# The routing's chain laid out in one piece, and long VectorE work of the attentions ordered behind its end

## The chip, the core and the metric

The kernel runs on one core of a Trainium2 chip. The metric is the device time of one execution in microseconds. A core has five engines that concern us: TensorE (PE in the profile, with its weight loads as PEld), VectorE (DVE), ScalarE (ACT), GpSimd (POOL) and SyncE (SP), which here only issues transfers. Each engine works through a queue of its own, fixed when the program is built.

## What is computed

Four macaron layers run over a residual stream of 4 batches of 1024 tokens with 128 channels, all in float32: half a feed-forward, an attention, the other half of the feed-forward. Layers 0 and 2 have a mixture of experts as their feed-forward, and these are where the change works. Cut to what matters:

```python
# layer 0; layer 2 is alike with relu and a router bias
logits = einsum('td,ed->te', layernorm(x), router_w)
top_vals, top_idx = top_k(logits, 2)                # 8 experts, two for each token
probs = softmax(top_vals)
out += probs[e] * (gelu(x @ w1[e].T + b1[e]) @ w2[e].T + b2[e])   # for the two chosen
x = x + 0.5 * out
# layer 0's attention: for each token, 16 heads of 8 channels attend to each other
scores = einsum('bshd,bstd->bsht', Q, K) / sqrt(8)
x = x + (softmax(scores) @ V) @ Wfc.T
# layer 2's attention: a linear recurrence over time with decay gamma
s = gamma * s + k_t v_t^T ; z = gamma * z + k_t ; y_t = q_t s / (q_t z + eps)
```

So a token's second routing (after the attention) can't be computed before its attention is done, and its attention not before its first experts are done.

## The kernel before

**Experts.** Only the chosen experts are computed. The tokens of a group of batches are sorted by expert into blocks of 128 slots: 23 blocks for a group of one batch, 39 for a group of two. For each block, `experts` (line 424) has SP load the expert's weights (0.58 MB, tile e_w, 4 buffers), has POOL gather the 128 tokens (L457, tile e_xg, 6 buffers), turns them on PE (L461), copies them on VectorE (L463, e_x), multiplies up, applies the activation on ScalarE (L468, e_h), multiplies down, adds the bias on VectorE (L441, e_y) and has POOL scatter the rows to DRAM (L442, res). `combine` (L476) loads the two rows of each token back (c_y), weighs them and adds them to the residual.

**Routing.** `route` (L276) says which token goes to which slot. It has a part for each batch (centring, squares, logits: L287 to L312), then a chain of small VectorE operations, each of which needs the one before: the two greatest logits (`top`, L321, tiles g_m to g_pick), counts per expert (L339 to L373), then, for 8 tokens of 128 at a time (g_lanes, L399), a comparison on VectorE and matmuls on PE that sum up which token stands in which slot (g_cols, held), and last g_source (L409), which the gathers read, and g_target (L412), which the scatters read. For two batches this chain is 50 VectorE instructions.

**Groups.** Layer 0 has six routings: batches (0), (1), (2,3) before the attention, (0,1), (2), (3) after it, with 23, 23, 39, 39, 23 and 23 blocks. Layer 2 has four of two batches each. I number the 326 blocks through: layer 0's second round begins with block 86, after (0), (1) and (2,3); its later groups begin with 125 and 148; layer 2's groups begin with 171, 210, 249 and 288. The routing of a group has to be done before its first block.

**Layout.** The functions are Python generators. `lanes` runs one lane of tasks for the experts, one for the combines, one or two for the rest, and always continues the lane whose clock is lowest; each `yield n` moves that lane's clock on by n. What stands in one stretch between two yields is laid out together. The order of layout is not yet the order on the engines: the framework's scheduler, which runs when the program is built, puts each engine's instructions in order by its own estimate of when each is ready, and prefers what was laid out earlier. After that the order on each engine is fixed, and semaphores wait where data come from another engine. A manual dependency marked NoSync adds only an order for the scheduler, no wait in the program.

In `route`, the first part yields 8 after each batch, and the chain yields 3, 5, 3, then 1 for each group of lanes, and 2 at the end, so that it can be interleaved with the other lanes' tasks.

**The attentions.** `l0_attn` (L501) works through 8 steps of 128 tokens per batch. A step has four long VectorE operations over 2048 elements per partition: q times k (L528, prod), the sum over channels (L530, sc), weights times values (L545, prod) and the sum over the attended heads (L547, o), and some six short ones. I call these four the long operations; layer 0 has 4 x 8 x 4 = 128 of them. `l2_attn` (L878) has shorter ones (kv L894, at L901, den L917).

## Time and profile before

| | |
|---|---|
| median of 3 runs | 3209.11 us (3207.99 to 3214.21) |
| the profiled execution | 3296.3 us, span of its instructions 3294.4 us |
| mean granted TensorE clock in it | 0.905 of full speed |
| busy: PE, VectorE, ScalarE, POOL | 2875.3, 1826.5, 1649.2, 807.0 us |
| layer 0 with its experts | about 0 to 940 us of the span |
| layer 1's attention | about 940 to 2040 us |
| layer 2 with its experts | about 2100 to 2790 us |
| layer 3 | from about 2790 us |

The profiled execution is 2.7% longer than the median run, so times read in it are compared with each other and with its own span. Percentages of busy time are averages over stages that have different limits; a stretch of the span is judged by what its engines do in it.

Where each group of blocks stands in the profiled execution (the end of g_target L412, the start of the first e_x L463, the end of the last e_y L441):

| group | blocks | g_target ends | first e_x | last e_y |
|---|---|---|---|---|
| layer 0, (0) | 1 to 23 | 46.8 | 50.0 | 144.7 |
| (1) | 24 to 46 | 79.0 | 142.8 | 235.4 |
| (2,3) | 47 to 85 | 177.7 | 232.6 | 386.7 |
| second round, (0,1) | 86 to 124 | 514.6 | 516.9 | 670.1 |
| (2) | 125 to 147 | 643.8 | 667.4 | 783.2 |
| (3) | 148 to 170 | 791.4 | 797.3 | 897.5 |
| layer 2, (0,1) | 171 to 209 | 2153.9 | 2159.3 | 2291.4 |
| (2,3) | 210 to 248 | 2215.3 | 2289.6 | 2450.9 |
| second round, (0,1) | 249 to 287 | 2476.2 | 2479.6 | 2646.8 |
| (2,3) | 288 to 326 | 2649.7 | 2653.9 | 2780.8 |

### The profile page before, as it was taken

The page shows a single profiled execution, that of the slowest core. Times are in us where ns is not written, and L with a number is a line of the kernel's source. Part 1 is how long each engine was busy: PE and PEld are TensorE (multiplying, and loading weights), DVE is VectorE, ACT ScalarE, POOL GpSimd, SP SyncE. Part 2 cuts the span into 40 slices and gives each one's busy share as a digit, 9 for nine tenths or more (in the row PEclk, how much of TensorE's full clock was granted, in tenths as well). Part 3 has the DMA queues.
Part 4 walks back from the last instruction along what each step waited for, and adds up shares of the span by engine and source line. Part 5 has one row for each costly group of instructions (what it writes and reads, how often), then busy time and mean ns, then how long its engine had stood idle before and what let it go on. Part 6 is the DMA issues. An engine that isn't in the chain of part 4 may idle for free.

```text
span 3294.4 us, 48535 instructions
## 1 busy us (share of the span) xinstructions
PE 2875.3 (87%) x18206; PEld 1685.8 (51%) x18206; DVE 1826.5 (55%) x3160; ACT 1649.2 (50%) x3640; POOL 807.0 (24%) x748
## 2 busy tenths in 40 slices
PE   6888637878879999999999999988988977899997
PEld 6766426766643333333333333586777865344333
DVE  3376877774226676676776772431555521355664
ACT  3565524658613565566566565444444534444442
POOL 2565405552340000000000000046434454011110
PEclk7989858889977999999999999979989988788997
DMA  4766414663500000000000000157565666000000
GB/s 151 227 186 188 140 42 130 185 188 115 168 9 7 4 6 4 6 6 4 21 5 6 1 1 9 42 152 245 171 185 147 199 197 194 0 0 0 7 7 13
DMA packets 122890, 277.64 MB, mean 84 GB/s; under 512 B 18016, under 2 KB 67296, under 8 KB 122528
## 3 DMA queue, kind: packets, MB, share of 16 engines
q1 hardware_dynamic: 101792, 231.77, 23.8%
q0 software_dynamic: 20864, 42.77, 4.3%
q8 instruction: 144, 2.36, 0.3%
q14 instruction: 90, 0.74, 0.1%
HBM read 238.43 MB, written 31.85 MB: 82 GB/s over the span
## 4 chain that ended last, share of the span: by engine, by line
PE 74%; DVE 12%; ACT 5%; issue 4%; DMA 3%; POOL 1%; another core or an unknown queue 0%; SPq 0%; ACTq 0%; DVEq 0%; POOLq 0%
PE bank L227 40%; PE two L227 17%; PE o L227 8%; PE s L227 4%; DVE nm L720 2%; ACT e_h L468 2%; PE wave L1010 1%; DVE prod L545 1%; PE bank L461 1%; DMA c_y<-res 1%; DVE sc L530 1%; ACT L468 1%; DMA e_w<-in_l0m_dram 1%; DVE prod L528 1%; DVE e_x L463 1%
## 5 line engine op out<-in xcount | busy, mean ns | idle before, releaser
L720 DVE TENSOR_REDUCE nm<-two 128x2 f32<-128x1024 f32 x512 | 626.9, 1225 | 288.3 <-PE s L227 268.9
L743 ACT ACTIVATE e<-s 128x512 f32<-128x512 f32 x1024 | 556.4, 595 | 405.6 <-PE s L227 402.6
L468 ACT ACTIVATE e_h<-bank,e_w 128x128 f32<-128x128 f32 x1304 | 454.8, 368 | 511.6 <-PE bank L227 388.4
L227 PE MATMUL bank<-e_x,e_w 128*128 128x128 f32 x2608 | 569.3, 318 | 154.5 <-ACT e_h L468 79.9
L227 PE MATMUL s<-qm,kz 32*128 32x512 f32 x2048 | 634.1, 643 | 0.8 <-ACT e L743 0.8
L227 PE MATMUL two<-kz,qz 32*128 32x512 f32 x2048 | 593.2, 664 | 21.3 <-DVE nm L720 2.5
L227 PEld LDWEIGHTS bank<-e_x,e_w 128*128 128x128 f32 x2608 | 413.9, 204 | 291.3 <-ACT e_h L468 144.4
L457 POOL DMA_INDIRECT e_xg<-rows,g_source x326 | 334.4, 1026 | 835.1 <-DVE g_target L412 354.2
L227 PE MATMUL bank<-e_w,e_h 128*128 128x128 f32 x2608 | 445.7, 291 | 12.3 <-ACT e_h L468 6.9
L442 POOL DMA_INDIRECT res<-e_y,g_target x326 | 373.5, 1146 | 337.0 <-DVE e_y L441 152.7
L227 PEld LDWEIGHTS bank<-e_w,e_h 128*128 128x128 f32 x2608 | 378.8, 205 | 23.0 <-ACT e_h L468 13.3
L227 PE MATMUL o<-e,va 128*32 128x256 f32 x4096 | 328.8, 392 | 0.1
L441 DVE TENSOR_TENSOR e_y<-bank,e_w 128x128 f32<-128x128 f32 x326 | 94.3, 290 | 403.7 <-PE bank L227 317.0
L227 PEld LDWEIGHTS two<-kz,qz 32*128 32x128 f32 x2048 | 159.7, 189 | 239.9 <-issue 164.0
L227 PEld LDWEIGHTS o<-e,va 128*32 128x32 f32 x4096 | 81.0, 108 | 390.3 <-issue 370.3
L227 PEld LDWEIGHTS s<-qm,kz 32*128 32x128 f32 x2048 | 206.9, 183 | 10.9 <-issue 7.7
L708 POOL COPY va<-vd 128x256 f32<-128x256 f32 x16 | 6.7, 433 | 626.3 <-PE o L227 538.0
L1115 POOL TENSOR_TENSOR z<-st,r 128x512 f32<-128x512 f32 x32 | 46.2, 1445 | 417.1 <-DVE st L1108 333.7
L463 DVE COPY e_x<-bank 128x128 f32<-128x128 f32 x326 | 93.0, 285 | 92.2 <-PE bank L461 67.6
L227 PE MATMUL bank<-g_cols,g_lanes 128*128 128x39 f32 (+1 forms) x512 | 90.5, 341 | 28.9 <-DVE g_cols L392 28.8
L461 PE MATMUL bank<-c,e_xg 128*128 128x128 f32 x326 | 95.0, 291 | 21.7 <-DMA e_xg<-rows,g_source 21.6
L227 PEld LDWEIGHTS bank<-g_cols,g_lanes 128*128 128x128 f32 x512 | 91.2, 270 | 32.5 <-issue 31.4
(300 smaller groups left out, 3694.0 us busy)
## 6 DMA issues: line engine op xcount, KB each, us to landing
e_w<-in_l0m_dram SPq DMA_DIRECT2D x170, 578.0 KB
e_w<-in_l2m_dram SPq DMA_DIRECT2D x156, 578.0 KB
c_y<-res SPq DMA_DIRECT2D x32, 512.0 KB
rows<-g_xt SPq DMA_DIRECT2D x16, 512.0 KB
e_xg<-rows,g_source POOLq DMA_INDIRECT x326
res<-e_y,g_target POOLq DMA_INDIRECT x326
x<-in_x_dram SPq DMA_DIRECT2D x4, 512.0 KB
qz<-qd SPq DMA_DIRECT2D x64, 32.0 KB
```

The costliest lines, as they stand in the source:

```text
L227: self.nc.tensor.matmul(out, lhsT, rhs, start=start, stop=stop)
L441: nc.vector.tensor_tensor(y, o, w[:, MOE_W - D :], ALU.add)
L442: ins = nc.gpsimd.indirect_dma_start(out=res[:, :], out_offset=at(target[:, k : k + 1]), in_=y, in_offset=None)
L457: nc.gpsimd.indirect_dma_start(out=xg, out_offset=None, in_=rows[:, :], in_offset=at(source[:, k : k + 1]))
L461: nc.tensor.transpose(tp, xg, self.c0["ident"])
L463: nc.vector.tensor_copy(x, tp)
L468: nc.scalar.activation(h[:, fc, :], up[:, fc, :], func, bias=w[:, 2 * FC * P + fc : 2 * FC * P + fc + 1])
L528: v.tensor_tensor(pr, q.unsqueeze(2).to_broadcast(sh), k.unsqueeze(1).to_broadcast(sh), ALU.mult)
L530: v.tensor_reduce(sc, pr, AX.X, ALU.add)
L720: v.tensor_reduce(nm[:, it, h, 2 * pair : 2 * pair + 2], s, AX.X, ALU.max, negate=True)
L743: nc.scalar.activation(es[g], s, AF.Exp, scale=scale)
L1115: (pool if i else v).tensor_tensor(z, st[:, 0:HALF], r, ALU.mult)
```

## The change

The inner yields of `route` are taken away. What is left are 13 after each batch's first part (8 before) and one of 25 at the end, so the chain is laid out in one stretch. A routing of one batch moves its lane's clock by 38 (25 before), one of two batches by 51 (37 before). The name of the instruction that makes g_target is kept as `self.fence`, and `behind` gives certain VectorE instructions of the attentions that are laid out later an order after it, without a wait: the four long ones of `l0_attn`, and kv, at and den of `l2_attn`.

```diff
--- before.py
+++ after.py
@@ -270,10 +270,17 @@
         self.nc.vector.reciprocal(r, std)
         return r
 
+    def behind(self, i):
+
+        if self.fence:
+            order = mybir.DependencyInfo(mybir.DependencyClass.NoSync, mybir.DependencyReason.DATA)
+            self.tc.add_manual_dep(i.ins, self.fence, order, reason="a routing is not cut up")
+
 
 
 
     def route(self, ps, wp, m, batches, out):
+
 
         nc, c0 = self.nc, self.c0
         v = nc.vector
@@ -309,7 +316,7 @@
             v.tensor_tensor(L[:, at], lp, r.unsqueeze(2).to_broadcast([P, NT, NE]), ALU.mult)
             if "rb" in m:
                 v.tensor_tensor(L[:, at], L[:, at], m["rb"].unsqueeze(1).to_broadcast([P, NT, NE]), ALU.add)
-            yield 8
+            yield 13
 
         full = [P, gt, NE]
         small = lambda tag: one([P, gt, 1], tag)
@@ -332,7 +339,6 @@
         L2 = one(full, "g_l2")
         v.scalar_tensor_tensor(L2, pick[:, 0], -3e38, L, ALU.mult, ALU.add)
         m2 = top(L2, 1)
-        yield 3
 
 
         taken = one([P, NE, gt], "g_taken")
@@ -371,7 +377,6 @@
         lane, col = one([P, 2 * gt, 1], "g_lane"), one([P, 2 * gt, 1], "g_col")
         v.tensor_copy(lane, lane_i)
         v.tensor_copy(col, col_i)
-        yield 5
 
 
         sh = [1, blocks, NE]
@@ -390,7 +395,6 @@
         cols = one(sh, "g_cols")
         v.tensor_tensor(cols, column.unsqueeze(1).to_broadcast(sh), col.to_broadcast(sh), ALU.is_equal)
         v.tensor_tensor(cols, cols, c0["token"][:, 0 : 2 * gt].unsqueeze(2).to_broadcast(sh), ALU.mult)
-        yield 3
         held = bank((P, blocks))
         for q in range(2 * gt // 4):
             sh = [P, 4, P]
@@ -400,7 +404,6 @@
             for j in range(4):
                 n = 4 * q + j
                 self.mm(held, lanes[:, j, :], cols[:, n, :], start=n == 0, stop=n == 2 * gt - 1)
-            yield 1
         U32 = mybir.dt.uint32
         w, far = one([P, blocks], "g_w"), one([P, blocks], "g_far")
         v.tensor_scalar(w, held, -1.0, None, ALU.add)
@@ -409,7 +412,7 @@
         v.scalar_tensor_tensor(source, w, 0.0, far, ALU.max, ALU.subtract)
         v.scalar_tensor_tensor(far, w, -0.5, c0[f"spare{len(batches)}"], ALU.is_lt, ALU.mult)
         target = one([P, blocks], "g_target", U32)
-        v.tensor_tensor(target, w, far, ALU.add)
+        self.fence = v.tensor_tensor(target, w, far, ALU.add).ins.name
 
         e = small("g_e")
         v.tensor_tensor(e, m2, m1, ALU.subtract)
@@ -419,7 +422,7 @@
         v.reciprocal(p1, p1)
         v.tensor_tensor(p2, e, p1, ALU.mult)
         out.update(rows=rows, source=source, target=target, expert=expert, p1=p1, p2=p2)
-        yield 2
+        yield 25
 
     def experts(self, ps, wp, weights, func, batches, plan):
 
@@ -525,9 +528,9 @@
             k = qkv[:, 1, :].rearrange("p (t d) -> p t d", d=HD)
             sh = [P, NH, NH, HD]
             pr = self.t(wp, sh, "prod", bufs=3)
-            v.tensor_tensor(pr, q.unsqueeze(2).to_broadcast(sh), k.unsqueeze(1).to_broadcast(sh), ALU.mult)
+            self.behind(v.tensor_tensor(pr, q.unsqueeze(2).to_broadcast(sh), k.unsqueeze(1).to_broadcast(sh), ALU.mult))
             sc = self.t(wp, [P, NH, NH], "sc")
-            v.tensor_reduce(sc, pr, AX.X, ALU.add)
+            self.behind(v.tensor_reduce(sc, pr, AX.X, ALU.add))
             mx = self.t(wp, [P, NH, 1], "mx")
             v.tensor_reduce(mx, sc, AX.X, ALU.max)
             v.tensor_tensor(sc, sc, mx.to_broadcast([P, NH, NH]), ALU.subtract)
@@ -542,9 +545,9 @@
             values = qkv[:, 2, :].rearrange("p (d t) -> p d t", d=HD)
             sh = [P, NH, HD, NH]
             pv = self.t(wp, sh, "prod", bufs=3)
-            v.tensor_tensor(pv, ex.unsqueeze(2).to_broadcast(sh), values.unsqueeze(1).to_broadcast(sh), ALU.mult)
+            self.behind(v.tensor_tensor(pv, ex.unsqueeze(2).to_broadcast(sh), values.unsqueeze(1).to_broadcast(sh), ALU.mult))
             o = self.t(wp, [P, NH, HD], "o")
-            v.tensor_reduce(o, pv, AX.X, ALU.add)
+            self.behind(v.tensor_reduce(o, pv, AX.X, ALU.add))
             v.tensor_tensor(o, o, sm.to_broadcast([P, NH, HD]), ALU.mult)
             return o.rearrange("p h d -> p (h d)")
 
@@ -891,14 +894,14 @@
             kvp = bank((P, 2 * D))
             self.mm(kvp, xn[:, c], m["wkv"])
             kv = self.t(wp, [P, 3 * D], "kv", bufs=3)
-            v.tensor_tensor(kv[:, 0 : 2 * D], m["bkv"], kvp, ALU.add)
+            self.behind(v.tensor_tensor(kv[:, 0 : 2 * D], m["bkv"], kvp, ALU.add))
             nc.vector.memset(kv[:, 2 * D :], 1.0)
             ks = self.t(wp, [P, D], "ks", bufs=3)
             v.tensor_scalar(ks, kv[:, 0:D], 0.0, G[:, P - 1 : P], ALU.max, ALU.mult)
             ap = bank((P, P))
             self.mm(ap, k[:, c], q[:, j, :])
             at = self.t(wp, [P, P], "at", bufs=3)
-            v.tensor_tensor(at, G, ap, ALU.mult)
+            self.behind(v.tensor_tensor(at, G, ap, ALU.mult))
             nd = bank((P, 2, P))
             for n in range(2):
                 self.mm(nd[:, n, :], kv[:, (1 + n) * D : (2 + n) * D], at, stop=state is None)
@@ -914,7 +917,7 @@
                     v.scalar_tensor_tensor(new, state, gp[:, 7:8], sp, ALU.mult, ALU.add)
                 state = new
             den = self.t(wp, [P, P], "den", bufs=3)
-            v.tensor_scalar(den, nd[:, 1, :], L2_EPS, None, ALU.add)
+            self.behind(v.tensor_scalar(den, nd[:, 1, :], L2_EPS, None, ALU.add))
             v.reciprocal(den, den)
             y = self.t(wp, [P, P], "y")
             v.tensor_tensor(y, den, nd[:, 0, :], ALU.mult)
@@ -1283,7 +1286,7 @@
 
     def run(self, stages):
         nc = self.nc
-        self.X = []
+        self.X, self.fence = [], None
         self.c0 = self.load("c0")
         for b in range(B):
             X = self.t(self.res, [P, S], f"x{b}")
```

## The prediction

> **What bounds the kernel now.** The page's slices first: PE is near full except in two places of the routed layers, and there its granted clock falls too. The table of busy time by stretch then shows the larger, the gap between block 85 and block 86 of layer 0, and two smaller ones (782 to 800, before block 148; 2450 to 2480, before block 249). VectorE's timeline says what stands in the gap.
>
> ```profile
> PE   6888637878879999999999999988988977899997
> DVE  3376877774226676676776772431555521355664
> 384.00:427.00 43.00, 10.43 (x30) 5.77 (x29) 37.64 (x50) 9.36 (x26) 1.43 (x2) 0.54 0.19 52
> 427.00:461.00 34.00, 22.74 (x90) 17.06 (x88) 16.61 (x20) 19.16 (x62) 0.00 (x0) 0.60 0.05 16
> 461.00:491.00 30.00, 3.16 (x8) 1.77 (x8) 29.23 (x55) 2.06 (x6) 0.00 (x0) 0.50 0.29 97
> 491.00:517.00 26.00, 17.94 (x72) 15.97 (x73) 19.06 (x25) 2.12 (x5) 3.79 (x3) 0.50 0.02 6
> 782.00:800.00 18.00, 14.19 (x79) 11.33 (x78) 9.65 (x26) 9.41 (x18) 7.41 (x8) 0.82 0.53 143
> 2450.00:2480.00 30.00, 17.10 (x77) 15.68 (x76) 16.59 (x45) 4.91 (x16) 4.97 (x5) 0.54 0.51 158
> ...
> 426.70 0.69 DVE L572 TENSOR_TENSOR x<-x,bank 128x512 f32<-128x512 f32 x1 [3.06 <-PE bank L227]
> 434.46 0.20 DVE L270 RECIPROCAL arstd<-astd 128x8 f32<-128x8 f32 x1 [7.08 <-ACT astd L268]
> 455.48 0.42 DVE L540 TENSOR_REDUCE sm<-ex 128x16 f32<-128x256 f32 x1 [7.83 <-ACT ex L535]
> 460.65 0.28 DVE L323 TENSOR_REDUCE g_m<-g_l 128x16 f32<-128x128 f32 x1
> 461.24 2.29 DVE L528 TENSOR_TENSOR prod<-qkv 128x2048 f32<-128x2048 f32 x1
> 463.44 0.29 DVE L325 TENSOR_TENSOR g_at<-g_at,c 128x128 f32<-128x128 f32 x1
> 463.64 2.28 DVE L530 TENSOR_REDUCE sc<-prod 128x256 f32<-128x2048 f32 x1
> ...
> 514.39 0.19 DVE L412 TENSOR_TENSOR g_target<-g_w,g_far 128x39 uint32<-128x39 f32 x1
> 514.72 2.28 DVE L528 TENSOR_TENSOR prod<-qkv 128x2048 f32<-128x2048 f32 x1
> 516.92 0.28 DVE L463 COPY e_x<-bank 128x128 f32<-128x128 f32 x1
> ```
>
> The columns after a stretch's length are busy us of PE, PEld, DVE, ACT and POOL, then granted clock, DMA share and GB/s. To be seen: from 384 to 517 VectorE works 102.5 of 133 us while PE mostly waits. It finishes batch 1's attention (residual added at 426.70), then from 460.65 to 514.6 runs the routing's chain with long attention operations of batch 2 between its short ones, and block 86 begins two operations later. The other two gaps differ: PE is busy 14.2 of 18 and 17.1 of 30 us in them, so only 3.8 and 12.9 us of PE are lost.
>
> **What the Trainium skill says.** "DVE: scalar operands, raw-bit mode, write accounting and state across instructions", section 5, states that VectorE's queue is one in-order queue. The trace agrees: at 455.48 everything waits 7.83 us behind one operand from ACT. So what counts is who stands ahead of whom. "VectorE: DVE Perf Modes", section "Mode 1×", gives one result per cycle, so 2048 elements at its 0.96 GHz would take an estimated 2.13 us; the trace has 2.28, and 2.20 from start to start, which I use. "TensorE: Matmul & The Clock Gate", "What's actually happening", says that an idle PE falls to half clock; the stretches with 0.50 agree, so a chain that runs alone has slow matmuls.
>
> **The change part by part.** The change adds and removes no VectorE instruction. The order of the two built programs shows what it moves; I count instructions there and price them with the rows above: long operation 2.20, short one 0.2 to 0.33, g_cols 1.37, g_lanes or a 512-wide addition 0.61, all start to start.
>
> *Layout costs.* A routing takes 13 or 14 more on its lane's clock, so attention 0 is laid out 11 blocks later: its first step ends at block 46 (37 before), its last at 73 (62), batch 1's first at 84 (72).
>
> *1, blocks 24 to 85.* 40 long operations stand there, not 51, so 2.75 steps less. Blocks 30 to 84 went at 3.8 us each with 12.75 steps among 54 of them; without attention, blocks 6 to 24 took about 3.5. That is 0.3 x 54 / 12.75, some 1.3 us a step, up to 1.9 if the undisturbed pace is 3.35: I take -5 us, between -15 and 0.
>
> *2, block 85's e_x to batch 1's residual.* 24 long and 58 short ones instead of 13 and 43: 70.5 us of VectorE against 42.1. Before, 5.3 us of waits lay in it, of which c_y's 2.2 are now covered: +26 (22 to 30).
>
> *3, from there to the chain's first g_m.* 10 long ones instead of 6, 27.0 us of work against 16.1, for batch 1's routing front is laid out one attention step later. The 7.83 us wait goes down to about 2: on ACT the two exponentials now stand before batch 1's squares. +5 (0 to 9).
>
> *4, the chain.* Between g_m and g_target 77 instructions stood, now 50, none foreign: 12 long (26.4 us) and 15 short (4.2) go. But some 7 us of these filled waits for PE's lane matmuls. The chain before block 249, nearly alone and also at half clock, took 2443.46 to 2476.2, 32.7 us with two e_x, four e_y and eight c_y in it; I take 31 instead of 54: -23 (-26 to -19).
>
> *5, g_target to block 86.* This is the new wait. The steps laid out after the chain and before the experts come due at once behind g_target, and they are ahead of e_x in the queue: eight long and six or seven short ones, 19.9 us, where two operations (2.6 us) stood. Behind the first e_x wait PE, ACT and all of block 86; POOL's gathers are hidden. +17 (14 to 18). What block 86 would wait for otherwise, its gather, needs 2.3 us after g_target and is covered.
>
> Sum so far: -5 + 26 + 5 - 23 + 17 = +20 for block 86.
>
> *6, blocks 86 to 139.* VectorE has 3 to 7 us more per five blocks up to 116 and as much less after; PE and VectorE have slack there (107.6 of 148 us busy from 521 to 669). 0 (-5 to +8).
>
> *7, the routing before block 148.* Its g_target moves from behind block 147's e_x to behind block 143's, so the wait of 7 us for it goes. But PE was busy 52 of 60 us from 740 to 800, with feed-forward of layer 1 that only changes places: at most 8 us can be had. The order of ACT shows 13 function-table loads fewer in all, 11 of them in blocks 148 to 170, since feed-forward and experts alternate less. "ScalarE: Activation LUTs", "What ACT_TABLE_LOAD costs", prices the load at about 1283 ns; the trace has 1.28 us. That is 14 us of ACT, but PE is busy 47.3 of 50 us from 800 to 850: I take 2. -10 (-18 to 0).
>
> *8, layer 2.* No attention operation stood inside its chains before, only e_x and e_y, so the fence does nothing there; the layout does. Before block 249, 65 VectorE instructions (20.9 us) stood between block 247's e_x and g_target, now 5. The gap's 12.9 us of idle PE are saved. Given back: POOL's scatters of blocks 247 and 248 now stand behind the gathers of blocks 254 and 256, which need the buffers that blocks 248 and 250 free, so combines 2 and 3 and their attentions come later against the blocks; and the routing before block 288 starts its chain at block 284 instead of 281 but ends at 287 as before. Only three blocks, 9 us of work, then cover 31 us of chain: about +9. The first routing of the layer ends three VectorE instructions and some 2 us of PE work later: +2. SP's loads of c_y stand behind three more e_w loads, inside the same delay. Together -1 (-10 to +10).
>
> Layers 1 and 3 keep their instructions. Total: +20 + 0 - 10 - 1 = +9 us on the profiled 3296.3, that is 3305. The median before was 2.7% lower than that execution; I put the same difference on it: 3209 + 9 = 3218.
>
> **The rivals.** *Slower still:* the eight operations, and then the denser VectorE queue up to block 116, delay the experts, and 7 brings nothing because batches 2's and 3's attentions trail: +20 + 6 - 0 + 2 = +28, 3237. For it: VectorE is ahead of PE in that window. Against: total VectorE work doesn't change. *Faster:* the routings before blocks 148 and 249 are ready before their blocks, and the visible waits go, 783.2 to 797.3 and 2450.9 to 2479.6, 43 us together, because the PE work in them finds room among the blocks. For it: both g_target now stand ahead of the group's last block. Against: PE is 90% busy from 740 to 782 and 95% from 2420 to 2450, so that work lengthens the blocks. It decides from half of the 43 us on, where it covers the +20 of block 86; at three quarters it gives +20 + 2 - 32 = -10, 3199. *No change:* the parts cancel within 6 us, 3209; or the fence is inert because the operations it holds would have been late anyway. The order shows that it isn't: the first chain after the attention has no foreign instruction left.
>
> **How the numbers follow.** 0.2% (6.4 us) is about what a measurement of this kernel can tell from no change. My forecast, 3218 with its own range of 3215 to 3228 gets 0.42; slower still 0.16; no change 0.16; faster 0.26. So slower 0.58, same 0.16, faster 0.26. The range leaves out about a tenth at each end: 3196 to 3240. Costs that the trace does not show are 3's wait and 8's give-back; both are in it.
>
> **What would show it.** In the profile after: g_target of the fourth routing (514.6 before) within 10 us of 517, but the first e_x behind it 18 to 21 us later with eight long operations between (step 5); batch 1's residual some 20 us later (1, 2); the chain in about 31 us without a prod in it (4); no idle stretch before blocks 148 and 249 (7, 8), and a longer one before 288. The forecast is wrong if block 86 starts less than 10 us later than before, or if layer 2 from block 210 to 326 is over 10 us shorter.

## The result, and the profile after

| | before | after |
|---|---|---|
| median (four runs each) | 3210.51 us | 3264.52 us (3262.08 to 3272.85) |
| ratio | | 1.0172, 95% interval 1.0150 to 1.0194 |
| the same two again, on two other occasions | | 1.0183 (1.0155 to 1.0211), 1.0161 (1.0140 to 1.0181) |

The change costs 54 us. The forecast was +9, with a range up to 3240: right in sign, and too small by 45 us.

The level of a kernel differs from one occasion to the next (the kernel before took 3285 and 3290 us in two of the sets of runs below, 3214 to 3215 in the other three), so everything that follows compares kernels of one set, or of sets at the same level, and the profile shown ahead of the prediction, which stood at the upper level, is not set against one of the lower. Both kernels were profiled again in one set, in executions of 3214.70 and 3267.22 us; what follows reads these two, called h1 (before) and h2 (after).

The page's slices first, two lines of h1, then of h2:

```profile
PE   7877547878879999999999999999989987899997
DVE  3387876864236776676777773452555522355764
```

```profile
PE   7888636879969999999999999989998987899997
DVE  3258887684325676676677673352554542355664
```

Slices of 82 us are too coarse: the gap of layer 0 is still in the fifth to seventh digits of PE and DVE, and little else can be seen. So I cut the span where the blocks do: windows from the first e_x of one group of blocks to that of the next, with one more window from the last e_y of block 85 to the first e_x of block 86, and one from the last e_y of block 170 to the first e_x of block 171. The kernel before, in the order blocks 1 to 23, 24 to 46, 47 to 85, the gap, 86 to 124, 125 to 147, 148 to 170, all of layer 1 up to block 171, blocks 171 to 326 (after the length: busy us of PE, PEld, DVE, ACT and POOL, granted clock, DMA share, GB/s):

```profile
49.40:124.30 74.90, 67.99 (x485) 63.04 (x485) 30.89 (x115) 48.55 (x148) 47.85 (x48) 0.91 0.73 219
124.30:218.20 93.90, 79.40 (x495) 67.26 (x496) 59.69 (x102) 53.03 (x126) 57.75 (x47) 0.89 0.60 189
218.20:370.70 152.50, 118.62 (x733) 97.12 (x733) 118.24 (x180) 95.28 (x218) 91.35 (x74) 0.93 0.59 185
370.70:497.30 126.60, 49.46 (x194) 37.16 (x195) 99.79 (x143) 30.41 (x96) 4.66 (x4) 0.55 0.15 46
497.30:640.00 142.70, 120.42 (x774) 101.21 (x773) 109.01 (x201) 96.50 (x231) 100.03 (x80) 0.92 0.61 194
640.00:769.20 129.20, 104.25 (x596) 82.33 (x596) 76.83 (x181) 85.11 (x190) 51.14 (x47) 0.88 0.55 168
769.20:864.50 95.30, 90.61 (x513) 67.27 (x512) 27.42 (x71) 72.50 (x133) 39.89 (x41) 0.98 0.48 148
864.50:2124.30 1259.80, 1204.46 (x9334) 473.43 (x9335) 767.00 (x827) 660.57 (x1243) 57.35 (x64) 0.95 0.05 10
2124.30:2699.30 575.00, 526.60 (x3635) 455.63 (x3635) 261.98 (x853) 278.18 (x827) 305.04 (x307) 0.95 0.66 208
```

The changed kernel, same windows:

```profile
49.70:112.40 62.70, 59.99 (x417) 51.86 (x417) 17.89 (x72) 32.29 (x91) 46.34 (x49) 1.00 0.78 248
112.40:225.60 113.20, 94.13 (x558) 84.87 (x558) 52.47 (x127) 61.97 (x172) 52.35 (x46) 0.79 0.51 163
225.60:374.40 148.80, 119.89 (x729) 98.04 (x727) 111.95 (x173) 93.30 (x216) 88.79 (x74) 0.91 0.60 191
374.40:528.60 154.20, 55.67 (x203) 40.10 (x203) 125.18 (x166) 36.41 (x106) 12.83 (x8) 0.56 0.13 40
528.60:689.80 161.20, 127.24 (x780) 106.09 (x781) 122.99 (x213) 99.72 (x236) 90.12 (x75) 0.88 0.54 169
689.80:802.60 112.80, 95.56 (x576) 77.02 (x575) 63.32 (x161) 76.34 (x175) 51.05 (x48) 0.92 0.58 177
802.60:904.70 102.10, 94.40 (x528) 68.99 (x526) 30.47 (x81) 66.65 (x136) 39.17 (x40) 0.98 0.50 155
904.70:2176.10 1271.40, 1210.58 (x9337) 475.94 (x9337) 770.28 (x839) 663.72 (x1256) 55.97 (x62) 0.95 0.04 10
2176.10:2751.10 575.00, 532.39 (x3631) 462.59 (x3631) 254.45 (x842) 271.86 (x811) 303.16 (x309) 0.95 0.66 209
```

Length against length: -12.2, +19.3, -3.7, +27.6, +18.5, -16.4, +6.8, +11.6, 0.0. The start of block 1 adds 0.3, and the sum is +51.8 us, nearly all of the 52.6 us by which the two spans differ. Three stretches lose most: blocks 24 to 46, the gap before block 86, and blocks 86 to 124. The second of these is what the forecast was made of. VectorE's column shows where work went: out of blocks 1 to 85, into the gap (+25.4) and into blocks 86 to 124 (+14.0), out of 125 to 147 (-13.5).

The gap, in VectorE's timeline (start, length, line, and in brackets the wait before it). The kernel before, residual of batch 1 (x), first step of the chain (g_m), its end (g_target) and block 86's e_x:

```profile
410.63 0.69 DVE L572 TENSOR_TENSOR x<-x,bank 128x512 f32<-128x512 f32 x1 [3.06 <-PE bank L227]
...
441.03 0.28 DVE L323 TENSOR_REDUCE g_m<-g_l 128x16 f32<-128x128 f32 x1
...
494.79 0.19 DVE L412 TENSOR_TENSOR g_target<-g_w,g_far 128x39 uint32<-128x39 f32 x1
...
497.31 0.28 DVE L463 COPY e_x<-bank 128x128 f32<-128x128 f32 x1
```

The changed kernel:

```profile
440.22 0.69 DVE L575 TENSOR_TENSOR x<-x,bank 128x512 f32<-128x512 f32 x1 [3.06 <-PE bank L227]
...
478.66 0.24 DVE L330 TENSOR_REDUCE g_m<-g_l 128x16 f32<-128x128 f32 x1
...
508.94 0.20 DVE L415 TENSOR_TENSOR g_target<-g_w,g_far 128x39 uint32<-128x39 f32 x1
509.06 2.29 DVE L531 TENSOR_TENSOR prod<-qkv 128x2048 f32<-128x2048 f32 x1
511.26 2.28 DVE L548 TENSOR_TENSOR prod<-ex,qkv 128x2048 f32<-128x2048 f32 x1
...
526.42 2.28 DVE L550 TENSOR_REDUCE o<-prod 128x128 f32<-128x2048 f32 x1
528.62 0.28 DVE L466 COPY e_x<-bank 128x128 f32<-128x128 f32 x1
```

The chain runs from 478.66 to 509.1 with no long operation in it, and behind g_target eight long ones stand before block 86's e_x.

### The profile page after: what moved, and what is told of

Same layout as the page of the kernel before. It is cut to its first block, busy times and chain, and to the rows that moved or that the text cites. A ratio compares the mean times of both kernels' runs of the same rounds, so it can differ in the third digit from the quotient of the medians.

```text
span 3260.3 us, 48547 instructions
## 1 busy us (share of the span) xinstructions
PE 2862.8 (88%) x18206; PEld 1679.9 (52%) x18206; DVE 1824.0 (56%) x3160; ACT 1630.2 (50%) x3627; POOL 789.2 (24%) x748
## 5 line engine op out<-in xcount | busy, mean ns | idle before, releaser
L227 PE MATMUL bank<-e_x,e_w 128*128 128x128 f32 x2608 | 563.5, 317 | 114.6 <-ACT e_h L471 45.7
L227 PEld LDWEIGHTS bank<-e_x,e_w 128*128 128x128 f32 x2608 | 408.7, 202 | 244.6 <-ACT e_h L471 104.7
L227 PE MATMUL bank<-e_w,e_h 128*128 128x128 f32 x2608 | 439.0, 287 | 4.3 <-ACT e_h L471 4.2
L445 POOL DMA_INDIRECT res<-e_y,g_target x326 | 359.2, 1102 | 264.8 <-DVE e_y L444 86.4
L227 PEld LDWEIGHTS bank<-e_w,e_h 128*128 128x128 f32 x2608 | 372.0, 202 | 11.1 <-ACT e_h L471 8.9
L227 PEld LDWEIGHTS s<-qm,kz 32*128 32x128 f32 x2048 | 207.1, 183 | 11.6 <-issue 7.7
```

The costliest lines, as they stand in the source:

```text
L227: self.nc.tensor.matmul(out, lhsT, rhs, start=start, stop=stop)
L445: ins = nc.gpsimd.indirect_dma_start(out=res[:, :], out_offset=at(target[:, k : k + 1]), in_=y, in_offset=None)
```

## The experiments

Lengths in us of all kernels profiled, by the same windows (171 to 326 in one). The first nine rows are read against h1, the others against e1, which stood at the upper level:

| kernel | 1-23 | 24-46 | 47-85 | gap | 86-124 | 125-147 | 148-170 | to 171 | 171-326 | ratio |
|---|---|---|---|---|---|---|---|---|---|---|
| before (h1) | 74.9 | 93.9 | 152.5 | 126.6 | 142.7 | 129.2 | 95.3 | 1259.8 | 575.0 | 1 |
| after (h2) | 62.7 | 113.2 | 148.8 | 154.2 | 161.2 | 112.8 | 102.1 | 1271.4 | 575.0 | 1.0161 |
| g1 | 76.2 | 81.4 | 151.8 | 129.3 | 160.9 | 113.5 | 99.7 | 1273.6 | 579.0 | 1.0024 |
| g2 | 63.2 | 104.7 | 144.6 | 154.9 | 146.0 | 128.9 | 94.0 | 1261.4 | 574.1 | 1.0051 |
| g3 | 73.2 | 100.2 | 176.2 | 126.4 | 145.9 | 114.5 | 97.8 | 1259.0 | 573.7 | 1.0045 |
| g4 | 76.4 | 98.3 | 185.2 | 105.0 | 171.6 | 117.3 | 97.0 | 1257.6 | 573.4 | 1.0102 |
| h3 | 63.6 | 113.8 | 147.0 | 156.0 | 143.4 | 128.9 | 93.6 | 1254.5 | 573.0 | 1.0086 |
| h4 | 76.2 | 82.2 | 151.5 | 130.1 | 143.6 | 128.7 | 95.8 | 1259.4 | 576.0 | 0.9965 |
| k1 | 63.3 | 114.0 | 147.0 | 155.6 | 161.1 | 113.5 | 100.0 | 1257.3 | 576.3 | 1.0125 |
| before (e1) | 88.8 | 86.3 | 153.9 | 126.7 | 149.1 | 129.5 | 101.7 | 1260.6 | 615.2 | 1 |
| e2 | 79.1 | 117.1 | 150.8 | 153.9 | 160.8 | 116.9 | 108.3 | 1273.5 | 609.3 | 1.0115 |
| e3 | 91.0 | 86.8 | 154.8 | 120.8 | 166.4 | 140.8 | 99.7 | 1255.7 | 620.0 | 1.0051 |
| e4 | 91.5 | 94.6 | 154.1 | 128.7 | 157.7 | 127.1 | 101.3 | 1262.3 | 611.2 | 1.0015 |
| after (f1) | 80.6 | 113.8 | 150.7 | 152.0 | 170.8 | 114.6 | 107.9 | 1271.4 | 614.9 | 1.0183 |
| f2 | 82.8 | 110.6 | 146.7 | 162.9 | 154.1 | 123.1 | 104.7 | 1270.3 | 638.6 | 1.0172 |
| f3 | 83.9 | 107.0 | 148.3 | 153.1 | 167.2 | 114.1 | 106.5 | 1272.0 | 615.8 | 1.0119 |
| f4 | 92.3 | 93.7 | 158.5 | 106.8 | 177.5 | 135.7 | 100.2 | 1254.6 | 629.4 | 1.0042 |

A stretch varies from one profile to the next: blocks 24 to 46 take 86.3 us in e1 and 94.6 in e4, though their VectorE does the same there. So a difference of one row is read only together with the ratio or with a second row.

**First set: the parts of the change.** Theory A puts the loss into layer 0, B into layer 2. C says that the raised clocks of the lanes are the loss, D that it is the eight long operations ahead of block 86. (Their microseconds are for a kernel before at 3210; read them as differences from it.)

The kernel before, unchanged:

> The kernel before, unchanged, for a profile that is not longer than its timed runs. Expected 3210 us, ratio 1.000. Theory A (the loss is made in layer 0): in this profile the blocks of layer 2 run at the same pace as in the profile after (2.7 to 2.8 us where nothing runs beside them), block 86 starts well ahead of 528 us and layer 0's last e_y ends some 40 to 50 us ahead of 910. Theory B (the loss is in layer 2, from the changed order around blocks 249 and 288): layer 0 ends within 15 us of 910 and layer 2 from block 171 to 326 takes 30 us or more less than the 571 us of after.

The changed kernel without the fence:

```diff
     def behind(self, i):
-        if self.fence:
+        if False and self.fence:
```

> The chain in one piece and the new yields of 13 and 25, but nothing ordered behind g_target. By the order of its instructions layer 2 is the same as after; attention 0 and 1 stand as late as after (steps end at blocks 46, 73, 84); only the fourth chain has 7 long operations in it again and 1 instead of 8 stands between g_target and block 86. Theory C (the raised lane clocks, which lay the attentions 11 blocks later, are the loss): 3255 to 3265, as after. Theory D (the eight long operations that the order puts ahead of block 86 are the loss): 3215 to 3245. Prediction's own sum: the eight cost 17, seven in the chain cost 15, so within 5 us of after.

The changed kernel with the old clocks: one piece and the fence stay, a routing moves its lane by the 25 and 37 of before.

```diff
-            yield 13
+            yield 8
...
-        yield 25
+        yield 13 + 2 * gt // 4
```

> The chain in one piece and the order behind g_target as after, but yields of 8 per batch and 17 or 21 at the end, so that a routing moves its lane's clock by 25 or 37 as before. The attentions stand at the same blocks as before (37, 62, 72), 13 long operations between block 85 and batch 1's residual as before, none in the fourth chain, eight between g_target and block 86. Theory C: within 10 us of before (3200 to 3220; the chain gives 23, the eight cost 17). Theory D: 3230 to 3265.

The fence alone, all yields as before:

```diff
-            yield 13
+            yield 8
...
+        yield 3
...
+        yield 5
...
-        yield 25
+        yield 2
```

> The yields of before, with the order behind g_target alone. Eight of the twelve long operations stay in the fourth chain, two stand between g_target and block 86. Theory C: the same as before within 6 us. Theory D: little of its cause is here, so also within 10 us of before; it tells whether the order by itself does harm where the layout is the old one.

Measured: e1 1.0000 (0.9984 to 1.0017), e2 1.0115 (1.0079 to 1.0152), e3 1.0051 (1.0035 to 1.0066), e4 1.0015 (0.9996 to 1.0033). e1's profile stood at the upper level, so it can't be set against the first profile of the changed kernel as A and B wanted. The pair h1 and h2 can: layer 0's last e_y ends at 864.5 us and then at 904.7, 40.2 us later, another 11.6 us go before block 171, and blocks 171 to 326 take the same 575.0 us. That is A for the most part. Neither C nor D comes out as written: e2 lies between C's range (as after) and D's, e3 between C's (within 10 us of before) and D's (20 us and more). Most of the loss needs no fence, and most of it goes with the old clocks, so the clocks carry more of it. The fence by itself can't be told from nothing; taken out of the changed kernel it gives back some 0.5 to 0.7% (1.0115 against 1.0161 to 1.0183, of other sets and with wide intervals). In e3 the gap shrinks by 6 us, for the chain's gain and the eight operations nearly cancel, but blocks 86 to 147 lose 28.6 us.

**Second set: where it sits.** In layer 0 blocks 24 to 46 lose about 27 us in f1 against e1, where the prediction expected a gain. By the static order the third routing (batches 2 and 3, needed from block 47 on) stood between blocks 17 and 31, with 40 instructions of others in its chain; in the changed kernel it stands between 33 and 36 with 7. Theory E: this lump starves the block stream. Theory F: the attention that is laid out 11 blocks later is the loss, wherever the chain stands.

> The changed kernel once more, so that its stages stand beside those of the others on one chip. Both theories: 1.015 to 1.020 of the time before. Both also expect blocks 24 to 46 at 4.9 to 5.1 us each (before, beside the first experiments: 3.8) and a TensorE clock of about 0.5 for some 15 to 20 us in the third routing's chain.

The raised clocks alone, chain cut up as before, no fence:

```diff
-            yield 8
+            yield 13
...
-        yield 2
+        yield 14 - gt // 2
```

> The raised lane clocks alone: 13 after each batch, the chain cut at its four old places with 3, 5, 3 and 1s and the rest of 25 at its end, no fence. The third routing's chain then stands between blocks 33 and 41 (changed kernel: 33 and 36, before: 17 and 31). Theory E (the third routing stands in a lump in the block stream, TensorE runs dry and its clock halves): part of the lump is gone, so 1.005 to 1.012 of the time before, and blocks 24 to 46 at 4.2 to 4.6 us. Theory F (the attention that is laid out 11 blocks later is the loss, wherever its chain stands): 1.014 to 1.018, with the loss showing after block 60, since attention 0 stands as in the changed kernel.

The changed kernel, its third routing alone cut up again (`cut` is true for batches (2, 3) of layer 0):

```diff
+        if cut:
+            yield 3
...
-        yield 25
+        yield 14 - gt // 2 if cut else 25
```

> The changed kernel with its clocks and its fence, but the third routing alone (batches 2 and 3) cut up at the four old places. E: block 47 starts 10 to 25 us sooner than in the changed kernel and the end follows: 1.008 to 1.013 of the time before. F: nothing gained, 1.015 to 1.020.

The kernel before with the fourth routing alone in one piece and fenced (`cut` is false for it), a pause of 2 behind it, and attention 2 a little sooner:

```diff
+        if cut:
+            yield 3
...
-        v.tensor_tensor(target, w, far, ALU.add)
+        i = v.tensor_tensor(target, w, far, ALU.add)
+        if not cut:
+            self.fence = i.ins.name
...
-            yield 11.2
+            yield 9 if b == 2 else 11.2
```

> All old yields and the chain in one piece and the fence for one routing only, the fourth (batches 0 and 1, after the attention), which then pauses 2 and not 25, so that block 86 is laid out ahead of the attention's next long operations; attention 2 pays 9 for a step instead of 11.2. E: blocks 1 to 85 stay as before, the chain gives its 20 us (54 to 31, two long operations between g_target and block 86 instead of eight), of which the later attention takes some back by block 148: 0.993 to 0.998. F: with attention 2 and 3 laid out 5 to 9 blocks later, what the chain gives is lost in blocks 86 to 148: 1.000 to 1.006.

Measured: f1 1.0183 (1.0155 to 1.0211), f2 1.0172 (1.0146 to 1.0197), f3 1.0119 (1.0091 to 1.0147), f4 1.0042 (1.0025 to 1.0060). Beside f1, E has f3's number and F has f2's and f4's, so neither is the whole. f3 gains 16 us on the median of f1, as E says, but block 47 starts only 3.8 us sooner, not 10 to 25; the profiled execution of f1 is 9 us shorter than its median, so the two profiles differ by no more than 6.2 us, and where the rest of the gain lies can't be read. f2 loses as much as the changed kernel, as F says, but partly elsewhere: its second routing of layer 2 ends only at 2365 us, with block 210 waiting for it, and blocks 171 to 326 take 638.6 us, a loss that the changed kernel doesn't have. f4 takes 19.9 us off the gap and has lost it all again by block 148: blocks 86 to 124 take 28.4 us more and 125 to 147 another 6.2.

**Third set: first three routings or later ones, and the lever the other way.** Theory G: the clocks of layer 0's first three routings are the loss, for they leave more attention to do when block 85 is done. Theory H: the loss comes from the later routings, and attention only changes its place.

The changed kernel with old clocks for the first three routings (`early` is true for (0), (1) and (2, 3) of layer 0):

```diff
-            yield 13
+            yield 8 if early else 13
...
-        yield 25
+        yield 13 + gt // 2 if early else 25
```

> The changed kernel, with the old lane clocks (8 after a batch, 13 plus a half for each 128 tokens after the chain) for layer 0's three routings ahead of the attention alone; from the fourth routing on all is laid out as in the changed kernel. Theory G (the raised clocks of the first three routings are the loss: they put the third routing and the first two attentions 11 blocks later): 1.001 to 1.006 of the time before, blocks 24 to 46 back at 3.8 to 4.1 us each, last e_y of block 85 to block 86 at 117 to 124 us. Theory H (the loss comes from the later routings: their clocks, one piece and the fence): 1.010 to 1.016.

The kernel before with raised clocks for the first three routings:

```diff
-            yield 8
+            yield 13 if early else 8
...
-        yield 2
+        yield 14 - gt // 2 if early else 2
```

> The counterpart: the kernel before, cut up as it was and with no fence, with the raised clocks (13 after a batch, 25 in the chain) for layer 0's first three routings alone. G: nearly the whole loss, 1.012 to 1.018; blocks 1 to 23 gain 6 to 10 us, blocks 24 to 46 lose 15 to 28, the way from block 85 to block 86 loses 20 to 36. H: 1.000 to 1.006.

The kernel before with the attentions of batches 0 and 1 laid out sooner:

```diff
-            yield 11.2
+            yield 9 if b < 2 else 11.2
```

> The kernel before, with one number changed the other way: an attention step of batches 0 and 1 pays 9 instead of 11.2, so that attention 1 has 4 and not 13 of its long operations left after block 85. G (what counts is how much attention is left when block 85 is done): 107 to 120 us instead of 127 from block 85 to block 86, blocks 47 to 85 longer by 0 to 8 us: 0.993 to 0.999. H: VectorE's work only changes its place, 0.999 to 1.004.

The same for three batches, together with the fourth routing in one piece:

```diff
-            yield 11.2
+            yield 8 if b < 3 else 11.2
```

> The kernel before, with a step of attentions 0, 1 and 2 paying 8 instead of 11.2, and the chain in one piece with the fence for the fourth routing alone (a pause of 2 behind it). By the layout attention 2 and 3 then stand no later than before (blocks 85 to 98, 105 to 133). G: 92 to 107 us from block 85 to block 86, blocks 86 to 148 within 8 us of before: 0.988 to 0.996. H: what the sooner attention and the chain give is lost in blocks 47 to 148, 0.999 to 1.006.

Measured: g1 1.0024 (1.0011 to 1.0037), g2 1.0051 (1.0035 to 1.0066), g3 1.0045 (1.0030 to 1.0060), g4 1.0102 (1.0082 to 1.0122). g1 has G's number, though not the gap that G gave (129.3 us instead of 117 to 124). g2 has H's number: the gap grows by 28.3 us as G says, but blocks 24 to 46 lose only 10.8, and blocks 1 to 85 together get 8.8 us shorter. g4 lies above what either expected, g3 above G's range and at the edge of H's. G falls there (in g3 the gap stays at 126.4 us, and blocks 24 to 85 take 30.0 us more), and in g4 H's "only changes its place" with it: attention put among the blocks can cost more than the time it takes. VectorE's busy time against the length of the same stretch, in stretches where attention's work is what changes:

| | stretch | VectorE, us | length, us |
|---|---|---|---|
| g3 against before | 24 to 85 | +22.6 | +30.0 |
| g4 against before | 24 to 85 | +27.7 | +37.1 |
| f4 against before (e1) | 86 to 124 | +19.2 | +28.4 |
| e3 against before (e1) | 86 to 124 | +14.0 | +17.3 |
| after against before | 86 to 124 | +14.0 | +18.5 |
| after against before | 125 to 147 | -13.5 | -16.4 |

That is 1.2 to 1.5 us for each us of VectorE, though VectorE is busy only 109 of 143 us in such a stretch. It does not hold for every stretch: in e3 blocks 125 to 147 hold as much VectorE work as in e1 (76.3 and 76.6 us) and take 11.3 us longer, and blocks 24 to 85, where the third routing moves in, hold 13.5 us less in g2 and in h2 than before and take 2.9 and 15.6 us longer. Nor is VectorE separated from what an attention's step brings along on PE and ACT (+6.8 and +3.2 us in blocks 86 to 124 of h2). g4 takes 33.8 us of VectorE out of the gap and gets 21.6 us for it.

**Fourth set: one piece at the old and at the new place.** What was missing: clocks of the first three routings 0.51%, all later routings 0.24% (g1, which has the one piece in the first three too), but 1.6 to 1.8% together. Theory I: the third routing's chain in one piece at its new place is the rest. Theory J: it costs nothing there, and the parts don't add up because they meet behind block 85.

> The kernel before, for its stages on the chip of the three others: 1.000 of the time before.

> The changed kernel, for its stages on the same chip: 1.015 to 1.020 of the time before under both theories.

g2, and the chain in one piece for the same three routings. By the static order every later routing stands as in the kernel before:

```diff
-        yield 3
+        if not early:
+            yield 3
...
-        yield 14 - gt // 2 if early else 2
+        yield 25 if early else 2
```

> The raised clocks and the chain in one piece for layer 0's first three routings alone; no fence, and everything from the fourth routing on as before (the static order of every later routing is that of the kernel before). It differs from the run with the raised clocks alone (1.0051) by the one piece. Theory I (the third routing's chain in one piece at its new place, blocks 33 to 36, stops the block stream for some 16 us at half the TensorE clock): 1.010 to 1.015 of the time before. Theory J (the one piece costs nothing there, and what is missing between 1.0051 plus 1.0024 and 1.0172 comes from raised first routings and the fence meeting behind block 85): 1.003 to 1.008.

The same with the old clocks:

```diff
-            yield 13 if early else 8
+            yield 8
...
-        yield 25 if early else 2
+        yield 13 + gt // 2 if early else 2
```

> The chain in one piece for the first three routings alone at the old clocks: the third then stands at blocks 17 to 25 with 17 other instructions in it, in the part of the stream before block 24 to which I give the loads of weights as the limit. I: the piece is harmless at this place, 0.998 to 1.003 of the time before. J: the same, 0.998 to 1.003; above 1.005, one piece costs wherever it stands and both are wrong on its place.

Measured: h3 1.0086 (1.0067 to 1.0104), h4 0.9965 (0.9953 to 0.9976). h3 lies between the two ranges: against g2 one piece at the new place costs 0.35%, 11 us, not the whole 1%. By the two intervals, which are of different sets, it can be 4 to 19 us. h4 misses below both: at the old place one piece *gains* 0.35%. So g1 hid a gain under a loss: its later routings cost 0.59% (1.0024 against 0.9965), and now the parts add up, 0.51 + 0.35 + 0.59 = 1.45% against the 1.61 (1.40 to 1.81) measured beside them. The sum doesn't need J, and doesn't rule it out. h4 is faster than both kernels, 3202.94 us against 3214.17 for the one before. In its profile the gain stands in blocks 24 to 46 (82.2 us against 93.9; 81.4 in g1). But e3, with the same three chains in one piece at the old clocks, shows none there against e1 (86.8 and 86.3), so the place of the gain is less sure than the gain.

How the one piece works can be seen by comparing h2 with g2, which has the same clocks for these routings and the chain cut up. (h3, which differs from g2 by the one piece alone, shows from 172 to 188 what h2 shows: 70 matmuls at a clock of 0.50.) Windows of the changed kernel, then of g2:

```profile
124.00:136.00 12.00, 9.65 (x45) 9.41 (x46) 3.57 (x10) 5.46 (x22) 0.67 (x1) 0.59 0.52 190
172.00:188.00 16.00, 16.00 (x73) 14.97 (x73) 4.51 (x12) 1.99 (x6) 1.68 (x2) 0.51 0.06 16
```

```profile
124.00:136.00 12.00, 10.03 (x47) 9.70 (x48) 3.57 (x10) 5.34 (x22) 0.22 (x1) 0.60 0.49 181
172.00:188.00 16.00, 16.00 (x128) 14.69 (x128) 5.90 (x16) 6.51 (x19) 10.51 (x10) 1.00 0.73 222
```

From 172 to 188 PE is busy throughout in both. But with the chain in one piece it does 73 matmuls at a clock of 0.51, 48 of them the lanes', and POOL and DMA stand nearly still: the blocks hardly move. Cut up, it does 128 at full clock, 54 of them the lanes'. PE's timeline shows the step into it, of the changed kernel and then of g2:

```profile
168.12 3.60 PE L227 MATMUL bank<-g_cols,g_lanes 128*128 128x39 f32 x16 [4.44 <-DVE g_cols L397]
171.53 0.77 PE L227 MATMUL bank<-e_x,e_w 128*128 128x128 f32 x2
172.09 3.47 PE L227 MATMUL bank<-g_cols,g_lanes 128*128 128x39 f32 x16
```

```profile
173.20 1.21 PE L227 MATMUL bank<-g_cols,g_lanes 128*128 128x39 f32 x10
174.24 0.69 PE L227 MATMUL bank<-e_x,e_w 128*128 128x128 f32 x4
```

In PE's queue the blocks' matmuls stand behind those of the lanes. PE idles 4.44 us for g_cols, then works the lanes off 16 at a time and later 8, some 0.22 us each; in g2 they come in shorter runs, 0.12 us each, between more matmuls of the experts. The low clock from 124 to 136 is in both, and is not in the kernel before (1.00 there), so it goes with the raised clocks; I take it for the later place of the batches' first parts, which was not tried. That the clock halves *because* PE idles or is fed small matmuls was not tried by itself.

**Last: layer 2.** Between layer 0's last block and block 171 the changed kernel loses 11.6 us. VectorE's timeline of the kernel before shows batch 1's logits (g_l) coming 18.1 us after batch 0's, with one residual addition between:

```profile
2063.88 0.19 DVE L309 TENSOR_TENSOR g_l<-bank,g_rstd 128x64 f32<-128x64 f32 x1
...
2073.94 0.69 DVE L249 SCALAR_TENSOR_TENSOR x<-bank,x 128x512 f32<-128x512 f32 x1 [1.82 <-PE bank L227]
...
2081.99 0.22 DVE L309 TENSOR_TENSOR g_l<-bank,g_rstd 128x64 f32<-128x64 f32 x1
```

In the changed kernel it is 29.4 us and two:

```profile
2105.76 0.19 DVE L316 TENSOR_TENSOR g_l<-bank,g_rstd 128x64 f32<-128x64 f32 x1
...
2115.82 0.69 DVE L249 SCALAR_TENSOR_TENSOR x<-bank,x 128x512 f32<-128x512 f32 x1 [1.82 <-PE bank L227]
...
2125.61 0.69 DVE L249 SCALAR_TENSOR_TENSOR x<-bank,x 128x512 f32<-128x512 f32 x1 [1.83 <-PE bank L227]
...
2135.17 0.22 DVE L316 TENSOR_TENSOR g_l<-bank,g_rstd 128x64 f32<-128x64 f32 x1
```

The 13 that the first batch's part now pays lets a further piece of another batch's feed-forward in ahead of the second part, and block 171 needs both. The spacing goes with the lane's clock: it is 31 us in f2, which has the raised clocks with the chain cut up and no fence, and 19.8 us in e3, which has one piece and fence at the old clocks. Theory K: this is a loss of its own; L: layer 2 is neutral as a whole. The last run takes layer 2 back to the kernel before and leaves layer 0 changed:

```diff
-            yield 13
+            yield 8 if cut else 13
...
-        yield 25
+        yield 2 if cut else 25
```

> The changed kernel in layer 0 and the kernel before in layer 2 (old clocks, chain cut up, no fence; the static order of layer 2's four routings is that of before). Theory K (the raised clock of layer 2's first batches lets the second routing's preparation in ahead of the first routing's chain, which costs 11.6 us between layer 0's last block and block 171; what follows in layer 2 cancels): 1.011 to 1.014 of the time before instead of 1.0161 to 1.0183. L (layer 2 is neutral as a whole): 1.0155 to 1.0185.

Measured: 1.0125 (1.0105 to 1.0145), the way to block 171 is back at 1257.3 us, and the logits are 18.1 us apart again. K holds; by the ratios (1.0161 to 1.0183, less 1.0125) layer 2 carries some 0.4 to 0.6%.

## Why the prediction was wrong

By its own steps, with the pair of one set (h1, h2):

| step | predicted | measured |
|---|---|---|
| blocks 1 to 23, with the start of block 1 | none | -11.9 (124.3, then 112.4) |
| 1, blocks 24 to 85, to block 85's e_x | -5 (-15 to 0) | +14.4 (239.1, then 253.5) |
| 2, to batch 1's residual | +26 | +27.1 (47.2, then 74.3) |
| 3, to g_m | +5 | +8.0 (30.4, then 38.4) |
| 4, the chain | -23 | -23.5 (53.8, then 30.3) |
| 5, g_target to block 86 | +17 | +17.2 (2.5, then 19.7) |
| 6, blocks 86 to 139 | 0 (-5 to +8) | +18.6 (209.8, then 228.4) |
| 7, blocks 140 to 147 | -10 | -16.5 (62.1, then 45.6) |
| blocks 148 to 170 | none | +6.8 |
| 8, the way to block 171 | +2 | +11.6 |
| 8, blocks 171 to 326 | -3 | 0.0 |
| sum | +9 | +51.8 |

*Right: 2 to 5.* The gap was worked out to within 4 us: the chain alone in 30 us, eight long operations in its place, and the attention that is left over. Step 3 came out 3 us high. The wait for ACT's ex (7.83 us in the forecast's profile, 6.83 in h1) did go, and 1.53 us for g_std were left; but the waits ahead of it, for astd and qkv, grew from 5.61 and 1.38 us to 6.97 and 2.45.

*Wrong: step 6, put at 0.* "PE and VectorE have slack there (107.6 of 148 us busy)" took an average for cover, and the 107.6 is VectorE's alone: PE was busy 121.1 of these 148 us. With 14 us more of VectorE, blocks 86 to 124 take 18.5 us more, nearly all of it by block 116 (115.9, then 133.7 us). Every block passes VectorE's in-order queue twice, at e_x and e_y, so a long operation ahead of either is on the block's path. PE's waits from block 86's first e_x to block 117's bear that out in part (us in total, times, longest; the first line is of the kernel before, the others of the changed one):

```profile
PE bank L227 <- DVE e_x L463: 4.5, 7, 1.2
PE bank L227 <- DVE e_x L466: 16.7, 7, 8.6
PE bank L568 <- DVE o L551: 6.2, 1, 6.2
```

The wait of 8.6 us is block 86's own and belongs to step 5, so 8.1 us stand against 4.5. The 6.2 us are a wait for an attention's result, ahead of block 113's matmuls in PE's queue. In all PE is idle 29.0 us there instead of 17.6, and busy 104.7 instead of 98.3 at a clock of 0.86 instead of 0.90, which the runs don't explain. The rival "slower still" named this place and gave it +6: its mechanism was right and its price a third of the measured one. Step 7 is the other side of it, and returned the more, but 148 to 170 took part of that back: the routing was ready at 786.5 us, and block 148 still started at 802.6, because block 147 came only at 796.7. The wait was replaced by late blocks.

*Wrong: step 1, by 19 us, which block 85's time hides.* Blocks 24 to 85 take 14.4 us more, not 5 less. That block 85 is only 2.5 us late is luck: blocks 1 to 23, at which the forecast didn't look, are 12.2 us shorter. The step looked at attention alone. The third routing moved as well, from blocks 17 to 31 to blocks 33 to 36, and there it stands in one piece: +11 us by the ratios of h3 and g2. With the chain cut up (g2) blocks 24 to 85 are still 2.9 us longer. The step's price for attention among the blocks, 1.3 us a step, is too low where g3 puts attention in: 9 long operations more in the static order of blocks 24 to 85 (8 in the profile), some 2.25 steps, go with 30 us, 13 a step. At that price the 2.75 steps that leave would have freed 36 us, and the third routing would have cost g2 39 us more there than before, against the 12 that it freed in blocks 1 to 23. No run moves the one without the other, so how much each does stays open.

*Wrong: step 8's "+2" for the first routing of layer 2.* It counted three VectorE instructions and 2 us of PE; what moved ahead of it was a piece of feed-forward, 9.8 us from one residual addition to the next. The rest of step 8 came out in kind: blocks 210 to 248 are 12.2 us shorter and 249 to 326 13.0 us longer, where the forecast had -12.9 and +9. (With the +2 its terms make -2, not the -1 that it put down.)

In the terms of the change, by the ratios: raised clocks ahead of the attention 16 us (g2), the chain in one piece at the place they give it 11 (h3 against g2), everything from the fourth routing on 19 (g1 against h4), of which layer 2 is perhaps the greater part (12 us by k1 against h2, 2 to 21 by their intervals). The chain's own gain, 23.5 us, is real and is spent where it arises, on the eight operations and on step 3. What is left open: the 0.2 to 0.4% between this sum and the ratios measured, which is within their intervals, the shares of attention and routing in blocks 24 to 85, and what makes the clock fall.

## What to carry to other kernels

A yield's number is part of the schedule: a change that lays a chain out in one stretch and also moves its lane's clock is two changes. Here the first alone, at the old clocks and for the three early routings, gains 0.35% (h4); for all routings, with the fence, it loses 0.51% (e3), and the raised clocks bring the loss to 1.6 to 1.8%. Don't take the slack of a stretch's average for cover when work moves into a stream of blocks: where attention was what moved here, the stretch grew by more than the full time of that work on the in-order queue that the blocks themselves need. And for each piece that is laid out later, ask what leaves the old place and what meets it at the new one: the third routing freed 12 us in blocks 1 to 23, where the forecast didn't look, and was in the way after them.

## What was not expected of the hardware

PE shown busy for a whole stretch did little more than half of the matmuls: 73 in 16 us at a clock of 0.51 against 128 at 1.00. The Trainium skill says in "TensorE: Matmul & The Clock Gate", "What's actually happening", that PE's clock is at half after an idle stretch and at full after some 3.4 us of sustained work. The trace agrees with the two speeds (a clock of 0.51 and 1.00, 0.22 and 0.12 us for a lane's matmul). But here the clock stayed at half for 16 us in which PE's record, whose ends of matmuls are modelled, shows no idle time at all, with 128x39 matmuls in long runs. A stretch's busy share has to be read together with its clock.
